# Another spacing of the edge stage's beats, and another order of loads, biases and accumulators in the first node tiles

## The chip, the cores and the metric

The kernel runs on one core of one Trainium2 chip, as one launch. The metric is the device time in microseconds (us). The core has five engines that are programmed apart and meet through semaphores: PE (matmuls), DVE (vector operations), ACT (activations), POOL (here mostly the issue of gathers and scatters) and SP (the issue of plain loads and stores).

## The reference, cut to what matters

The program is two layers on 625 nodes of 1024 numbers and 10000 edges. The change lies in layer 0 alone: a graph attention in 256 hidden numbers and four heads, a linear attention beside it, and a small quantised feed-forward block.

```python
def L0_gnn(x, edge_index, rms_w, W_down, Wl, Wr, att, W_up):
    x = x * rsqrt(mean(x * x) + 1e-6) * rms_w @ W_down
    src, dst = edges and one self loop a node
    xl, xr = (x @ Wl).reshape(n, 4, 64), (x @ Wr).reshape(n, 4, 64)
    msg = xl[src] + xr[dst]
    e = einsum('ehd,hd->eh', where(msg > 0, msg, 0.2 * msg), att)
    alpha = softmax of e over the edges of one dst
    return segment_sum(alpha[..., None] * xl[src], dst).reshape(n, 256) @ W_up

def L0_mix(x, ...):                      # linear attention, 16 heads of 64
    q, k, v = elu(x @ W_q + b_q) + 1, elu(x @ W_k + b_k) + 1, x @ W_v + b_v
    kv, ksum = einsum('bhnd,bhne->bhde', k, v), k.sum(axis=2)
    return (q @ kv / (q @ ksum + 1e-6)) @ W_o + b_o

def L0_ffn(x, w_gate, w_up, w_down):     # activations quantised by row, weights to -1, 0, 1
    return bitlinear(silu(bitlinear(x, w_gate)) * bitlinear(x, w_up), w_down)

xn = layernorm(x)
x = x + L0_gnn(xn, ...) + L0_mix(xn, ...)
x = x + L0_ffn(layernorm(x), ...)
# layer 1 follows: graph convolution twice, linear attention, latent attention, 8 experts of which 2
```

## The kernel before, in words

The nodes are five tiles of 125 (`NT` and `P`). Inside the part that the change touches the order on every engine is the order in which the program is written: `do(prep, pe, after, after2)` emits a group of matmuls and puts off what follows it on DVE and ACT to the next one or two calls of `do`. So a line that stands earlier in the program stands earlier in the queue of its engine, and an engine works its queue in order.

**The edge stage.** The edges are cut into chunks of 128, 79 in all (`EN`), in 40 groups of two (`groups`; the last has one chunk of 16 edges). For each chunk POOL gathers the rows `xl[src]` (L621, tile `ga`) and `xr[dst]` (L621, tile `gb`). For each group DVE adds them, applies the rectifier and `att`, and sums by head (`score_group`, L631 and L601 to L604). ACT takes the exp (L608). For each chunk POOL then scatters the four numbers an edge into `table`, a matrix in DRAM by source and destination (L641). The scatters all write `table`, so each waits until the one before has landed.

How often each pair of nodes occurs is counted meanwhile on PE from one-hot rows that DVE makes (`count`), into `CT`. Attention then needs no edges any more: it multiplies tiles of `table` by tiles of `CT`.

The edge stage runs beside the matmuls of the linear attention: keys and values in two halves (`lin.key`, `lin.value`), then queries and answers (`lin.query`, `lin.answer`), then the output projection (`mixed`, accumulators `px`). Each of these calls `work(us)` with an estimate of its matmul time. When the sum passes the next threshold, `one_beat` emits one beat: it is here that the gathers of group g, the scores of group g - `lags[0]`, the exp of group g - `lags[1]` and the scatters of group g - `lags[2]` are put into the queues, in this order:

```python
                for j in range(G):
                    if g < len(groups):
                        gather(g, j, 0)
                        scatter(g - lags[2] - 1)
                        gather(g, j, 1)
                    scatter(g - lags[2])
```

`scatter` takes the next chunk of the list if its group is old enough, and does nothing otherwise. The first gather of a beat waits for the last matmul that was emitted before it (`behind(got, latest["pe"])`); this is called its gate. The thresholds are 5.2 us apart for six beats and 8.6 after. The lags are 4, 5 and 6 groups, and 1, 1 and 2 from the output projection on; there two scatters fit between the gathers of one `j`, until the backlog is gone. Beats that are left when the matmuls run out follow in `while chunks: one_beat()`, behind the ternary weights of the feed-forward block (`ternary`, three operations on DVE for each of three matrices).

The loads of weights are issued by SP, each behind a matmul group: `lin.ahead[0].load()`, `wo[-1].load()` and `raw` after `lin.answer(m)`. The second half of tile 2's projection, `mixed(2, cs=(1,))`, is put behind the last scatter: it runs once the table is complete.

**The node tiles.** Then come seven periods, `p` from 0 to 6. SP and ACT load `table` by tiles (`load_table(t)`, tile `tb`) and SP the rows of x. In period p: `weigh(p + 1)` multiplies a table tile by the counts (L876, tile `pT`), `sums(p)` and `turn_sums(p)` make the attention's output, `up_again(p)` multiplies it by `W_up` on top of `px` of this tile, and L944 adds it to x. The feed-forward block of tile p - 1 goes through its steps `p1`, `f1` to `f4`, `p5` and `f5`; `f4` is the matmul with `w_down` into `pdn`, and L1042 adds it to x. `add_bias` adds the bias rows `bo` to x (L1069), and for tile 3 the finished projection `kept`. Tile 4's projection is made in period 1 in two halves, and `in_degrees` counts the edges of each node into `pdeg` in period 2.

The accumulators are three pairs of banks (`ps2`: `px`, `pdn`, `pdeg` among others) and two single banks (`ps1`). SBUF holds four tiles of the kind `mid`, which `tb`, `pT`, `kept` and later `kf` and `v` share.

Of the kernel before, what the change touches and what calls it, by code (L numbers as in the profile page):

```python
# [21 lines left out]
P = 125  # L22
# [31 lines left out]
def attempt(ctx: ExitStack, tc: tile.TileContext, w: dict, out: bass.AP, shifted: bool):  # L54
# [8 lines left out]
    def ps1(name):  # L63
        pool, n = psums[-1]
        return pool.tile([128, 512], FP, tag="ps1", name=name, bufs=n)

    def ps2(name):
        return psums[-1][0].tile([128, 2, 512], FP, tag="ps2", name=name, bufs=3)
# [294 lines left out]
    with ExitStack() as st0:  # L363
# [8 lines left out]
        with ExitStack() as edges:  # L372
# [305 lines left out]

            beat = dict(us=0.0, g=0, scored=0, raised=0)
            lags = [4, 5, 6]

            def scores(last):
# [10 lines left out]
            def one_beat():  # L695
                g = beat["g"]
                beat["g"] += 1
                if 5 <= g < NT + 5:
                    self_loops(g - 5)
                if lags[1] > lags[0]:  # L700
                    raise_all(g - lags[1])
                    scores(g - lags[0])
                else:
                    scores(g - lags[0])
                    raise_all(g - lags[1])
# [7 lines that stand above are left out]
            def work(us):  # L713
                beat["us"] += us

                while beat["us"] >= 2.0 + 5.2 * min(beat["g"], 6) + 8.6 * max(beat["g"] - 6, 0) and chunks:
                    one_beat()

            work(0.0)
            states = []  # L720
# [81 lines left out]
            def ternary(i):  # L802
# [4 lines left out]
                nc.vector.tensor_scalar(m, v.rearrange("p (k n) -> p k n", k=m.shape[1]), MAGIC, None,  # L807
                                        op0=ALU.subtract)

            for m in range(KC):  # L810
                if m + 1 < KC:
                    lin.query(m + 1)
                else:
                    mixed(0, range(6), paced=False)
                lin.answer(m, oT)
                if m < 2:
                    lin.ahead[0].load()
                elif m < 6:
                    if m % 2 == 0:
                        wo.append(Half(wpool, w["L0_Wo"], m // 2 - 1, now=False))  # L820
                    wo[-1].load()
                if m < 3:

                    raw.append(mid([128, 2 * D], "raw"))
                    behind(nc.sync.dma_start(out=raw[m].rearrange("p (k n) -> p k n", n=(256, 256, D)[m]),
                                             in_=w[("w_gate", "w_up", "w_down")[m]]
                                             .rearrange("(k p) n -> p k n", p=128)), latest["pe"])
# [3 lines left out]
            dn = mix.tile([128, 2, D], BF, tag="kv", name="dn", bufs=2)  # L831
            gu = wpool.tile([128, KC, 512], BF, tag="w", name="gu", padded_shape=[128, KC, 512])
            made = [gu[:, :, 0:256], gu[:, :, 256:512], dn]
            lags[:] = 1, 1, 2
            kept = mid([P, 2, 512], "kept")
            mixed(3, keep=kept, then=weight_sums)
            mixed(0, range(6, KC))
# [137 lines left out]
        def ffn(t):  # L975

            room = late.tile([128, 1536], FP, tag="room", name="room", bufs=1)
            xq = room[:P, 0:D]
            qT = room[:, D:D + KC * 64].bitcast(BF).rearrange("p (k n) -> p k n", k=KC)
            sg = room[:P, 0:256]  # L980
            hT = room[:, 256:384].bitcast(BF).rearrange("p (k n) -> p k n", k=2)
            xn1 = [mix.tile([128, NP], FP, tag="qf", name="xn1", bufs=2)[:P, 0:512] for h in range(2)]

            def p1():
                stats(t, mv0, rs0)
                nc.vector.tensor_scalar(xq, x[:, t, :], mv0[:, t, 0:1], rs0[:, t:t + 1],
                                        op0=ALU.subtract, op1=ALU.mult)
                quantise(xq, xq, rx[:, t:t + 1])

            def f1():  # L990
                def pe():
                    for h in range(2):
                        p = ps1("ptr").rearrange("p (c n) -> p c n", c=4)
                        for c in range(4):
                            k = 4 * h + c
                            nc.tensor.transpose(p[:, c, :P], xq[:, k * 128:(k + 1) * 128], ident[:P, :P])
                        nc.vector.tensor_scalar(qT[:, 4 * h:4 * h + 4, 0:P], p[:, :, :P], MAGIC, None,
                                                op0=ALU.subtract)

                do(None, pe)  # L1000

            def f2():
                def pe():
                    hold["pgu"] = ps2("pgu")[:, 0, :] if t == NT - 1 else ps1("pgu")
                    group(hold["pgu"][:P], [(qT[:, k, 0:P], gu[:, k, :]) for k in range(KC)])

                def after():
                    pgu = hold["pgu"]
                    rgu = late.tile([P, 2], FP, tag="rgu", name="rgu", bufs=2)

                    nc.vector.tensor_scalar(rgu, wmean[:P, 0:2], rx[:, t:t + 1], None, op0=ALU.mult)
                    nc.vector.tensor_scalar(rgu[:, 0:1], rgu[:, 0:1], 0.5, None, op0=ALU.mult)
                    nc.scalar.activation(sg, pgu[:P, 0:256], AF.Tanh, scale=rgu[:, 0:1])
                    nc.vector.scalar_tensor_tensor(sg, sg, 1.0, pgu[:P, 0:256], op0=ALU.add, op1=ALU.mult)
                    nc.vector.tensor_tensor(rgu[:, 1:2], rgu[:, 0:1], rgu[:, 1:2], op=ALU.mult)
                    nc.vector.scalar_tensor_tensor(sg, pgu[:P, 256:512], rgu[:, 1:2], sg, op0=ALU.mult, op1=ALU.mult)
                    quantise(sg, sg, rh[:, t:t + 1])

                do(None, pe, after)

            def f3():
                def pe():
                    ph = ps1("phT").rearrange("p (c n) -> p c n", c=4)
                    for c in range(2):
                        nc.tensor.transpose(ph[:, c, :P], sg[:, c * 128:(c + 1) * 128], ident[:P, :P])
                    nc.vector.tensor_scalar(hT[:, :, 0:P], ph[:, 0:2, :P], MAGIC, None, op0=ALU.subtract)

                do(None, pe)

            def f4():  # L1030
                def pe():
                    hold["pdn"] = ps2("pdn")
                    for c in range(2):
                        group(hold["pdn"][:P, c, :], [(hT[:, k, 0:P], dn[:, k, c * 512:(c + 1) * 512])
                                                   for k in range(2)])

                def after():
                    rd = late.tile([P, 1], FP, tag="rd", name="rd", bufs=2)
                    nc.vector.tensor_scalar(rd, wmean[:P, 2:3], rh[:, t:t + 1], None, op0=ALU.mult)
                    for c in range(2):  # L1040
                        xc = x[:, t, c * 512:(c + 1) * 512]
                        nc.vector.scalar_tensor_tensor(xc, hold["pdn"][:P, c, :], rd, xc, op0=ALU.mult, op1=ALU.add)  # L1042

                do(None, pe, after)

            def p5():
                stats(t, mv1, rs1)
                for h in range(2):
                    nc.vector.tensor_scalar(xn1[h], x[:, t, h * 512:(h + 1) * 512], mv1[:, t, 0:1], rs1[:, t:t + 1],
                                            op0=ALU.subtract, op1=ALU.mult)  # L1050

            def f5():
                def pe():
                    for h in range(2):
                        p = ps1("ptr").rearrange("p (c n) -> p c n", c=4)
                        for c in range(4):
                            nc.tensor.transpose(p[:, c, :P], xn1[h][:, c * 128:(c + 1) * 128], ident[:P, :P])
                        nc.scalar.activation(xnT1[:, 4 * h:4 * h + 4, nodes(t)], p[:, :, :P], AF.Copy)  # L1058

                do(None, pe)  # L1060

            return p1, f1, f2, f3, f4, p5, f5
# [8 lines left out]
        load_table(0)  # L1071
        for t in range(NT):
            rows_dma(nc.sync, x[:, t, :], xrows[t])
            if t == 1:
                load_table(1)
        weigh(0)
        add_bias(0, 1)
        kv_pieces = iter([(f, t) for t in range(NT) for f in ("key", "value")])
        made_of = {}

# [15 lines left out]
        for p in range(NT + 2):  # L1096
# [3 lines left out]
            if 1 <= p <= NT:  # L1100
                made_of[p - 1] = ffn(p - 1)
                made_of[p - 1][0]()
            if p == 1:
                mixed(4, cs=(0,))
            if p == 2:
                add_bias(2, 4)
                in_degrees()
            if p >= 3:
                spacer()
# [22 lines left out]
                weigh(p + 1)  # L1132
            if p + 2 < NT:
                load_table(p + 2)
            if p == 1:
                add_bias(3)
            if p == 1:
                mixed(4, cs=(1,))
                lin1.weights(0)
# [868 lines left out]
```

## Time and profile before

| | us |
|---|---|
| median of three runs | 2176.61 (2176.5 to 2177.32) |
| profiled execution, whole | 2173.66 |
| profiled execution, span from the first to the last instruction | 2171.8 |
| PE busy | 2094.0 (96% of the span) |
| DVE busy | 711.9 |
| POOL busy | 328.4 |
| ACT busy | 194.8 |
| edge stage, from the first gather to the last scatter | 51.97 to 404.85 |
| seven periods of node tiles | 405.9 to about 599 |

All times inside the execution are counted from its first instruction. The table is read so: PE works nearly all the time, so the end of the program moves by what PE waits less or more; busy time of the other engines counts only where PE waits for them. Durations come from the one profiled execution, and are compared with its own time.

A beat is named by its group number g, from 0. In the program before, beats 26 to 35 stand in the queries, beats 36 to 39 in the output projection and two more, with scatters alone, behind the ternary weights.

### The profile page before, as it was taken

To read this page: it belongs to the slowest core of one execution; us is meant where nothing else is said; L and a number is where in the kernel's file an instruction comes from. 1 tells how busy PE (TensorE), PEld (TensorE's weight loads), DVE (VectorE), ACT (ScalarE), POOL (GpSimd) and SP (SyncE) were. 2 spreads that over 40 slices of the span, in tenths; PEclk is the share of its full clock that TensorE was granted. 3 is DMA by queue.
4 is the path that set the end of the run, shared out by engine and by line. 5 is a ranking of instruction groups with operands and counts; after the bars stand their busy time and mean duration, and the time that the engine had idled before them with its cause. 6 is when DMAs were issued, how large, how long until landed. Compare 5 with 4: busy or idle time off the path is not lost. (4 is left out here: it accounts for less than half of the span.)

```text
span 2171.8 us, 17390 instructions
## 1 busy us (share of the span) xinstructions
PE 2094.0 (96%) x6934; PEld 1198.0 (55%) x6934; DVE 711.9 (33%) x1214; ACT 194.8 (9%) x355; POOL 328.4 (15%) x329
## 2 busy tenths in 40 slices
PE   8999999499999999999999999999999999999998
PEld 6665674255446677744446776467644444444443
DVE  5786486666443720000031334212111111111012
ACT  2000110012111100000000111110000000000000
POOL 1777766200000202010000000100000000000011
PEclk9999999699999999999999999999999999999999
DMA  7632362440302202131203101122299978997832
GB/s 224 206 112 83 118 199 75 120 134 1 120 6 78 84 5 87 49 136 42 75 1 125 59 0 40 35 90 97 82 366 342 328 276 323 330 328 265 293 136 86
DMA packets 147925, 301.63 MB, mean 139 GB/s; under 512 B 12411, under 2 KB 25602, under 8 KB 147830
## 3 DMA queue, kind: packets, MB, share of 16 engines
q1 hardware_dynamic: 127548, 252.54, 33.1%
q0 software_dynamic: 15296, 37.61, 5.5%
q10 hardware_dynamic: 4986, 10.22, 1.5%
q8 instruction: 58, 0.95, 0.2%
q14 instruction: 37, 0.30, 0.0%
HBM read 277.49 MB, written 22.84 MB: 138 GB/s over the span
## 5 line engine op out<-in xcount | busy, mean ns | idle before, releaser
L137 PE MATMUL pu<-w,xgT 128*128 128x512 f32 x768 | 333.9, 593 | 1.9 <-DVE xgT L1302 1.9
L137 PEld LDWEIGHTS pu<-w,xgT 128*128 128x128 f32 x768 | 144.0, 190 | 174.8 <-issue 172.0
L137 PE MATMUL pyb<-w,hb 128*128 128x512 f32 x384 | 174.3, 598 | 2.5 <-ACT yb L105 2.1
L137 PE MATMUL pk<-w,xnT 128*125 128x512 f32 x320 | 143.7, 603 | 2.2 <-ACT xnT L1058 2.2
L137 PE MATMUL pv<-w,xnT 128*125 128x512 f32 x320 | 140.8, 593 | 0.9 <-DVE x L944 0.9
L137 PE MATMUL pq<-xnT,w 128*128 128x313 f32 x512 | 139.3, 431 | 1.0 <-DVE v L293 0.8
L137 PE MATMUL p<-tT,w 128*128 128x313 f32 x512 | 136.3, 428 | 0.4 <-DVE tT L1302 0.4
L137 PEld LDWEIGHTS pq<-xnT,w 128*128 128x128 f32 x512 | 97.8, 192 | 40.5 <-DVE v L293 1.6
L137 PEld LDWEIGHTS pyb<-w,hb 128*128 128x128 f32 x384 | 69.8, 189 | 90.9 <-issue 74.8
L1842 DVE TENSOR_TENSOR su<-pu,su 128x512 f32<-128x512 f32 x24 | 16.6, 691 | 314.6 <-ACT su L1841 314.6
L137 PEld LDWEIGHTS p<-tT,w 128*128 128x128 f32 x512 | 96.8, 190 | 37.9 <-issue 1.2
L137 PEld LDWEIGHTS pk<-w,xnT 128*125 128x125 f32 x320 | 60.3, 191 | 76.0 <-issue 73.3
L765 PE MATMUL px<-w,oT 128*125 128x512 f32 x160 | 72.5, 611 | 30.9 <-DMA table<-es,at 28.4
L137 PEld LDWEIGHTS pv<-w,xnT 128*125 128x125 f32 x320 | 59.5, 188 | 73.5 <-issue 71.2
L641 POOL DMA_INDIRECT table<-es,at x79 | 83.8, 1061 | 56.4 <-issue 26.7
L1825 POOL DMA_INDIRECT xg<-rows_d,slots x12 | 11.3, 945 | 524.8 <-PE pxg L1832 449.0
L621 POOL DMA_INDIRECT ga<-xl_d,si x79 | 81.3, 1030 | 30.2 <-issue 21.7
L621 POOL DMA_INDIRECT gb<-xr_d,di x79 | 80.5, 1019 | 25.3 <-issue 23.5
L1191 DVE TENSOR_TENSOR z<-pz,z 125x512 fp32r<-125x512 f32 x10 | 6.9, 692 | 196.8 <-ACT z L1189 196.8
L137 PE MATMUL px<-w,hT 128*125 128x512 f32 x160 | 70.3, 592 | 0.0
L137 PE MATMUL px<-w,oT 128*125 128x512 f32 x160 | 70.3, 592 | 0.0
L137 PE MATMUL ph<-meanT,w 128*128 128x313 f32 x256 | 70.1, 426 | 0.0
(362 smaller groups left out, 2478.4 us busy)
## 6 DMA issues: line engine op xcount, KB each, us to landing
w<-in_eW_dram SPq DMA_DIRECT2D x144, 1024.0 KB
w<-in_L_Wk_dram SPq DMA_DIRECT2D x8, 1024.0 KB
w<-in_L_Wv_dram SPq DMA_DIRECT2D x8, 1024.0 KB
w<-in_L_Wq_dram SPq DMA_DIRECT2D x8, 1024.0 KB
w<-in_L_Wo_dram SPq DMA_DIRECT2D x8, 1024.0 KB
w<-in_W_self_dram SPq DMA_DIRECT2D x8, 1024.0 KB
w<-in_W_neigh_dram SPq DMA_DIRECT2D x8, 1024.0 KB
w<-in_sW_dram SPq DMA_DIRECT2D x8, 1024.0 KB
```

The source lines that it names most:

```text
L137: made = nc.tensor.matmul(dst, lhsT=lhsT, rhs=rhs, start=(i == 0), stop=(i == len(pairs) - 1))
L621: got = nc.gpsimd.indirect_dma_start(out=ab[g][side][0:p, j, :], out_offset=None, in_=src[:, :], in_offset=bass.IndirectOffsetOnAxis(ap=ix ...
L641: put = nc.gpsimd.indirect_dma_start(out=table[:, :], out_offset=bass.IndirectOffsetOnAxis(ap=at[0:p, lo + j:lo + j + 1], axis=0), in_=es[ ...
L765: made = nc.tensor.matmul(hold["px", t][:P, c, :], lhsT=oT[:, k, nodes(t)], rhs=wo[c](k), start=(k == 0), stop=(k == KC - 1 and keep is no ...
L1191: nc.vector.tensor_tensor(low, src, high.bitcast(FP), op=ALU.subtract)
L1825: nc.gpsimd.indirect_dma_start(out=xg, out_offset=None, in_=rows_d[:, :], in_offset=bass.IndirectOffsetOnAxis(ap=slots[:, b:b + 1], axis=0))
L1842: nc.vector.tensor_tensor(su, pu[:, 0, :], su, op=ALU.mult)
```

## The change

It has five parts.

- The thresholds of the beats: the next one is kept in `beat["next"]`. After six beats they are 8.3 us apart while keys and values are made, 8.6 in the queries, 7.0 in the output projection.
- The last lags are 1, 1 and 1.
- `load_table(1)` is issued after the rows of tile 0 instead of after those of tile 1.
- The biases of tiles 1 to 4 are all added in period 1, behind `p1` of tile 0; before, tile 1's stood ahead of the periods, tile 3's later in period 1 and those of tiles 2 and 4 in period 2.
- In `f4` tile 0 takes two single banks for `pdn` instead of a pair.

In the order of the program this moves beats 10 to 40 forward in part: beats 22 to 24 by one key or value, beat 27 from query 1 to the states before it, beats 28 and 29 by one query each, beats 32 to 34 likewise, beat 36 from tile 3's projection to `answer(6)`, beats 37 to 39 by half a tile's projection or one. Beat 36, which had the short lags before, has the long ones now. The two beats that stood behind the ternary weights become one with two scatters inside tile 1's projection, one with two inside tile 2's, and one with a single scatter at the end.

```diff
-            beat = dict(us=0.0, g=0, scored=0, raised=0)
+            beat = dict(us=0.0, next=2.0, apart=8.3, g=0, scored=0, raised=0)
...
             def work(us):
                 beat["us"] += us
 
-                while beat["us"] >= 2.0 + 5.2 * min(beat["g"], 6) + 8.6 * max(beat["g"] - 6, 0) and chunks:
+                while beat["us"] >= beat["next"] and chunks:
                     one_beat()
+                    beat["next"] += 5.2 if beat["g"] <= 6 else beat["apart"]
...
+            beat["apart"] = 8.6
             for m in range(KC):
                 if m + 1 < KC:
                     lin.query(m + 1)
...
-            lags[:] = 1, 1, 2
+            lags[:] = 1, 1, 1
+            beat["apart"] = 7.0
             kept = mid([P, 2, 512], "kept")
...
             def f4():
                 def pe():
-                    hold["pdn"] = ps2("pdn")
+                    if t:
+                        both = ps2("pdn")
+                        hold["pdn"] = [both[:P, c, :] for c in range(2)]
+                    else:
+                        hold["pdn"] = [ps1("pdn1")[:P] for c in range(2)]
                     for c in range(2):
-                        group(hold["pdn"][:P, c, :], [(hT[:, k, 0:P], dn[:, k, c * 512:(c + 1) * 512])
+                        group(hold["pdn"][c], [(hT[:, k, 0:P], dn[:, k, c * 512:(c + 1) * 512])
                                                    for k in range(2)])
...
         load_table(0)
         for t in range(NT):
             rows_dma(nc.sync, x[:, t, :], xrows[t])
-            if t == 1:
+            if t == 0:
                 load_table(1)
         weigh(0)
-        add_bias(0, 1)
+        add_bias(0)
...
             if p == 1:
+                add_bias(1, 2, 3, 4)
                 mixed(4, cs=(0,))
             if p == 2:
-                add_bias(2, 4)
                 in_degrees()
...
-            if p == 1:
-                add_bias(3)
             if p == 1:
                 mixed(4, cs=(1,))
                 lin1.weights(0)
```

More of the change, by code (lines that the diff above doesn't have):

```diff
@@ L1041, in after @@
                         xc = x[:, t, c * 512:(c + 1) * 512]
-                        nc.vector.scalar_tensor_tensor(xc, hold["pdn"][:P, c, :], rd, xc, op0=ALU.mult, op1=ALU.add)
+                        nc.vector.scalar_tensor_tensor(xc, hold["pdn"][c], rd, xc, op0=ALU.mult, op1=ALU.add)
                 do(None, pe, after)
```

## The prediction

> **What bounds the kernel now.** I read the busy shares first (PE 96%), then the waits of PE, because only time in which PE stands still can be won. Each line names who waited, for what, the sum, the times and the longest, in us.
>
> ```profile
> PE px L765 <- DMA table<-es,at: 28.4, 1, 28.4
> PE px L765 <- DVE x L944: 2.4, 1, 2.4
> PE pdeg L137 <- DVE x L1042: 1.5, 1, 1.5
> PE pdn L137 <- DVE x L944: 1.3, 1, 1.3
> ```
>
> The 28.4 is the edge stage: tile 2's second half cannot start before the last of 79 scatters has landed. The other three lie in the first node tiles. These four are what the change can reach.
>
> Next the timeline of POOL, which issues the edge stage's 158 gathers and 79 scatters (start, length, idle before and who ended it), with the SP queue's timeline at the same place.
>
> ```profile
> 261.93 0.96 POOL L621 DMA_INDIRECT ga<-xl_d,si  x1 [0.48 <-PE pq L137]
> ...
> 264.45 0.98 POOL L641 DMA_INDIRECT table<-es,at  x1 [0.30 <-issue]
> ...
> 270.75 1.40 POOL L641 DMA_INDIRECT table<-es,at  x1 [2.80 <-DVE ga L631]
> 272.47 0.96 POOL L621 DMA_INDIRECT ga<-xl_d,si  x1 [0.32 <-PE pq L137]
> ```
>
> ```profile
> 263.80 0.37 SPq L124 DMA_DIRECT2D w<-in_L_Wq_dram  x1
> 264.26 0.47 SPq L825 DMA_DIRECT2D raw<-in_w_gate_dram  x1
> ```
>
> A gather costs 0.96 and a gap of 0.30, a scatter 0.98 and 0.30; a beat of two times "gather, gather, scatter" is 7.62. Every scatter also waits until the scatter before has landed, since both write `table`. Two 1 MB loads start at 263.8, the scatter of 264.45 lands behind them, and the next goes at 270.75 instead of 268.28. The same is seen after the loads at 274.3, 284.9 and four later ones. Almost no gather waits for its PE gate: after 76 us the first gathers of beats 27, 28 and 29 alone are put down to PE, and POOL would have been free 0.18, 0.02 and 0.01 before them (the end of the scatter before, plus 0.30). So POOL's issues and landings set the pace, not the beats.
>
> The end of the stage, same timeline:
>
> ```profile
> 345.61 0.99 POOL L641 DMA_INDIRECT table<-es,at  x1 [0.30 <-issue]
> 346.90 0.96 POOL L621 DMA_INDIRECT ga<-xl_d,si  x1 [0.30 <-issue]
> 348.51 0.98 POOL L641 DMA_INDIRECT table<-es,at  x1 [0.65 <-issue]
> ...
> 387.77 2.17 POOL L641 DMA_INDIRECT table<-es,at  x1 [0.30 <-issue]
> 391.85 1.81 POOL L641 DMA_INDIRECT table<-es,at  x1 [1.91 <-issue]
> ...
> 398.78 0.96 POOL L641 DMA_INDIRECT table<-es,at  x1 [1.88 <-issue]
> 401.13 0.96 POOL L641 DMA_INDIRECT table<-es,at  x1 [1.40 <-DMA table<-es,at]
> 404.00 0.85 POOL L641 DMA_INDIRECT table<-es,at  x1 [1.91 <-issue]
> ```
>
> From beat 36 (346.90) scatters and gathers alternate; there the landing sets the interval between scatters and the gather between is free. After the last gather (385.19) six scatters go alone, 2.61 apart at the end, 3.74 while DVE's ternaries run (384.83 to 396.07).
>
> Last, DVE in the first node tile:
>
> ```profile
> 417.67 0.69 DVE L1069 TENSOR_TENSOR x<-x,bk_t 125x512 f32<-125x512 f32 x1 [0.99 <-DMA x<-in_x_dram]
> ...
> 423.20 4.89 DVE L876 TENSOR_TENSOR pT<-tb,CT 125x500 f32<-125x500 f32 x5 [2.48 <-DMA tb<-table]
> 427.99 1.23 DVE L944 TENSOR_TENSOR x<-px,x 125x1024 f32<-125x1024 f32 x1
> ```
>
> The second table tile lands at 423.20; `weigh(1)` holds DVE until 428.0; L944, whose input PE had ready at 426.83, comes behind it and gives back the accumulator for which tile 4's matmuls (429.28) wait.
>
> **What the Trainium skill says.** "DMA: Bandwidth & Descriptors", section "Anatomy of one DMA", puts the fixed cost of a POOL-issued DMA at about 2.0 us, mostly the receipt: the trace has 2.1 us to landing as the median for the scatters, and up to 6.3 beside loads. Its section "Issuing engines are not separate DMA queues" says that all queues interleave on the same 16 engines; the 2.5 us lost at 264.45 agrees. "SBUF — State Buffer", section "SBUF: two separate sides", says that a DVE operation in a two-port mode keeps GpSimd from writing descriptors; the trace agrees, with issues of 2.27, 2.17, 1.81 and 1.83 beside the ternaries. "PSUM — Partial Sum Buffer", section "Specifications", has eight banks per partition: three pairs and two singles fill them, so a fourth pair must wait for one to come free, as `pdn` does here (1.3).
>
> **The change, part by part.** *Beats.* The number of gathers, scatters and DVE operations stays. In program order beats 27 to 29 move up one query each, beat 36 moves from tile 3's matmuls to `answer(6)`, and the last ones follow. What this takes away is the gate: 0.2 us by the three numbers above. The loads hang on PE and stay, and a scatter behind a load leaves when the load is done, however early it came; that fixes POOL's time again at each load. Only a scatter that slips ahead of a load wins, a whole 3.81; it needs POOL about 2.3 us earlier there, and from 225.22 to 260.46 all slowdown together is 0.95 (35.24 against nine times 3.81). I take 0 for this, with 0 to -7.6 as bounds (two such slips). So beat 36 starts at 346.7 to 346.9 as before.
>
> *Last lags.* Beat 36 now comes before the lags are shortened and keeps "gather, gather, scatter". Its scatters go at +2.54 and +6.36 instead of +1.61 and +4.50, and the next at 356.15 instead of 354.31: 1.84 later. Seventeen scatters are then left in either kernel, two more of them alone (eight after the last gather, not six): alternating, an interval is 2.82 (348.51 to 383.81, twelve, less one stall of 1.51), alone 2.61, so 0.4 is won. Together with the gates: 1.84 - 0.4 - 0.2 = **+1.2**. Group 39's scores no longer stand behind the ternaries; that saves nothing, since its exp was ready at 397.7 and its scatter went at 404.00. The ternaries now wait for gather 39, which I put near 383, and start near 385 as before; their cost on POOL I keep, with -2 to +7 as bounds (nothing overlapped more; all 11.3 us of them overlapped, of which 4.5 is paid already). New wait: beat 38's scores stand before `kept` on DVE and wait for gather 37 (some 366), so `kept` ends near 370 instead of 363.6; tile 2's first half waits for that accumulator from 370.5. If it is late, the 28 us wait covers it.
>
> *Loads.* The two table DMAs of `load_table(1)` pass x tile 1's two on SP. Tile 1 took 2.28 us to land after tile 0 (417.67 - 415.39), so the table lands 2.3 earlier, at 420.9, and x tiles 1 to 4 up to 5.5 later (estimate: tile 4 at 430, used at 437). `weigh(1)` ends at 425.8, L944 starts when PE is done (426.87), tile 4's matmuls at 428.16: **-1.12**.
>
> *Biases.* Ten DVE additions, 0.61 apart, eight of them now together behind tile 0's quantising: 433.5 to 438.4, where DVE idled 6.1 us until `dens` (440.76, then 439.6). Cost nothing; if tile 4 landed after 438, it would delay `dens` by as much. Gone are two ahead of hT's copy (L1026) and four at 466.9 to 469.4, which held nobody. `kept` comes free earlier, so table tile 3 takes its place and waits for the additions (438.4) instead of PE (440.7); POOL's two bias loads (63.6 us of waiting) and the memset behind move from 469 to 439. Nothing waits for these before 478.
>
> *Accumulators.* For tile 0 `pdn` gets the single banks of `pgoT` and `phT`, the latter free with hT's copy, for which it waits anyway (452.5 now). It follows `px` at 3.44, as at 482.43 to 485.87: 453.67 instead of 456.26, of which 1.12 is counted: **-1.47**. `pdeg` then takes the pair of `px` 1, free when L944 ends (455.1) instead of L1042 (458.74): 455.15 instead of 458.79, **-1.05** more. Next in line are the transposes of `xn1`; DVE has those ready at 459.6, PE needs them at 462.2. From there PE has waits of 0.6 at most for two tiles, so the 3.64 reaches the end.
>
> Sum: 1.2 - 3.64 = -2.4. The profiled execution took 2173.66 (span 2171.8 and 1.9 around it), hence 2171.3; the three runs' median, 2176.61, lies 2.95 above it, hence 2174.2. About 0.2%, 4.35 us, is what a measurement of this kernel tells from no change.
>
> **Rivals.** *One: a scatter slips ahead of a load.* For it: one slip keeps its 3.81, and the old gates at beats 27 to 29 would have taken it back. Against it: 0.95 us to win, 2.3 needed. One slip gives -6.2, two -10.0; middle 2169.0. *Two: the lone scatters meet the ternaries and end slower than before.* Place: POOL, 378 to 406. Each lone scatter beside ternaries costs 3.74 instead of 2.61. It decides from 2.4 us, that is two more scatters caught; at four more it is +4.5 - 2.4 = +2.1, 2178.7, at the bound +7 - 2.4 = +4.6. Against it: DVE starts the ternaries at nearly the same time. *Three: the node tiles' waits move on instead of going* (DVE's stats before tile 1's transposes become the bound) and the change does nothing there: +1.2, 2177.8. Against it: 2.6 us of slack.
>
> **Chances.** Forecast 0.52 (2171.5 to 2176, a tenth of it below -4.35), one 0.29, two 0.12 (a third of it above +4.35), three 0.07. Faster 0.34, same 0.61, slower 0.05. The range, 2166.5 to 2178.5, takes in two slips and most of rival two.
>
> **What would show it.** Right: gathers still put down to "issue" at 260 to 345; beat 36 within 1 us of 346.9; eight lone scatters; the last scatter near 405; PE's waits on L944 near 1.3 and none for `pdn`; `pdeg` 3.6 earlier after the stage's end. Wrong: the last scatter before 402, or PE waits elsewhere between 455 and 500.

## The result, and the profile after

| | kernel before | changed kernel |
|---|---|---|
| median of 20 runs each, us | 2176.56 (2172.33 to 2180.14) | 2171.19 (2167.68 to 2176.42) |
| ratio | | 0.9976, 95% interval 0.9969 to 0.9984 |
| profiled execution, whole, us | 2173.66 | 2175.02 |

The change makes the kernel faster by about 5 us (5.4 by the medians). The profiled execution of the changed kernel is one of its longer ones, so the two profiles do not show that gain as a difference of their ends. They are compared by stage, each from its own mark: the first gather, and **M**, PE's start on tile 2's second half, right after the last scatter (405.94 before, 407.87 after). A time written M+17.46 is one 17.46 us after M in its own execution.

First the waits of PE from 400 to 520 us, after (who waited, for what; sum, times, longest):

```profile
PE px L766 <- DMA table<-es,at: 28.0, 1, 28.0
PE px L766 <- DVE x L947: 2.6, 1, 2.6
...
PE pg L137 <- ACT xnT L1065: 1.3, 2, 1.1
...
PE pdeg L137 <- DVE x L947: 0.5, 1, 0.5
```

Of the four waits shown before, that of `pdn` (1.3) is gone and that of `pdeg` is cut from 1.5 to 0.5. The one for L944 (now L947) stays: 2.6 against 2.4. A new one has come up, for ACT's copy of the transposes, 1.1 against 0.4 at its longest.

The timeline of POOL after, from beat 36 on (start, length, idle before and who ended it):

```profile
348.70 0.97 POOL L621 DMA_INDIRECT ga<-xl_d,si  x1 [0.30 <-issue]
...
356.07 1.36 POOL L641 DMA_INDIRECT table<-es,at  x1 [0.30 <-issue]
357.73 0.96 POOL L621 DMA_INDIRECT ga<-xl_d,si  x1 [0.30 <-issue]
359.34 1.16 POOL L641 DMA_INDIRECT table<-es,at  x1 [0.65 <-issue]
...
382.67 0.86 POOL L621 DMA_INDIRECT gb<-xr_d,di  x1 [0.31 <-issue]
383.83 1.00 POOL L641 DMA_INDIRECT table<-es,at  x1 [0.30 <-DMA table<-es,at]
386.76 2.28 POOL L641 DMA_INDIRECT table<-es,at  x1 [1.93 <-ACT es L608]
...
405.94 0.85 POOL L641 DMA_INDIRECT table<-es,at  x1 [1.91 <-issue]
```

The last gather is at 382.67 instead of 385.19, and eight scatters follow alone instead of six. The last scatter comes 1.94 later, of which 0.48 is a later first gather (52.45 against 51.97).

DVE after, in the first node tile:

```profile
425.33 4.87 DVE L879 TENSOR_TENSOR pT<-tb,CT 125x500 f32<-125x500 f32 x5 [2.64 <-DMA tb<-table]
430.11 1.22 DVE L947 TENSOR_TENSOR x<-px,x 125x1024 f32<-125x1024 f32 x1
```

Table tile 1 lands at M+17.46 (before: 423.20, M+17.26), though its DMAs now stand ahead of x tile 1's. L947 is as late as it was. SP's queue shows how little the new place is worth: the two DMAs of table tile 1 are issued at M+6.86 before (412.80) and at M+6.09 after (413.96), 0.77 earlier.

```profile
412.80 0.87 SPq L180 DMA_DIRECT2D tb<-table  x2
```

```profile
413.96 0.85 SPq L180 DMA_DIRECT2D tb<-table  x2
```

PE in period 2, first before, then after:

```profile
456.26 1.02 PE L137 MATMUL pdn<-dn,room 128*125 128x512 bf16 x4 [1.31 <-DVE x L944]
458.79 7.17 PE L137 MATMUL pdeg<-CT,ones 125*128 125x313 f32 x20 [1.50 <-DVE x L1042]
465.80 1.02 PE L1057 MATMUL ptr<-ident,xn 125*128 125x125 f32 x8
467.23 4.58 PE L137 MATMUL pg<-xl,pT 125*125 125x65 f32 x40 [0.41 <-ACT xnT L1058]
...
475.35 7.03 PE L137 MATMUL pk<-w,xnT 128*125 128x512 f32 x16
```

```profile
456.89 1.03 PE L137 MATMUL pdn<-dn,room 128*125 128x512 bf16 x4
458.37 5.54 PE L137 MATMUL pdeg<-CT,ones 125*128 125x313 f32 x20 [0.45 <-DVE x L947]
463.75 1.02 PE L1064 MATMUL ptr<-ident,xn 125*128 125x125 f32 x8
465.85 7.10 PE L137 MATMUL pg<-xl,pT 125*125 125x65 f32 x40 [1.08 <-ACT xnT L1065]
...
474.83 3.37 PE L137 MATMUL pgu<-gu,room 128*125 128x512 bf16 x8
...
478.25 7.03 PE L137 MATMUL pk<-w,xnT 128*125 128x512 f32 x16
```

From M, `pdn` starts 1.30 earlier than before and `pdeg` 2.35 earlier. `pdeg` also runs in 5.54 us instead of 7.17. Then `pg` takes 7.10 us and `pgu` 3.37; the windows view says why (window, its length; busy time and instructions of PE, PEld, DVE, ACT and POOL; granted PE clock, DMA share, GB/s):

```profile
470.00:480.00 10.00, 9.82 (x38) 7.00 (x38) 3.60 (x11) 2.03 (x3) 0.00 (x0) 0.61 0.50 125
467.57:477.81 10.24, 10.06 (x42) 8.29 (x41) 3.04 (x8) 1.28 (x1) 0.00 (x0) 0.50 0.38 100
```

PE was granted 0.61 of its clock over those 10 us, and half of it from 467.57 to 477.81. `pk` (478.25) starts 70.38 after M, against 69.41 before: in this execution the clock has taken back all that the accumulators had won.

### The profile page after: what moved, and what is told of

The parts are those of the page before. It is cut to its first block, busy times and chain, and to the rows that moved or that the text cites. A ratio compares the mean times of both kernels' runs of the same rounds, so it can differ in the third digit from the quotient of the medians.

```text
span 2173.3 us, 17398 instructions
## 1 busy us (share of the span) xinstructions
PE 2096.6 (96%) x6934; PEld 1202.3 (55%) x6934; DVE 712.4 (33%) x1214; ACT 194.4 (9%) x355; POOL 327.6 (15%) x329
## 5 line engine op out<-in xcount | busy, mean ns | idle before, releaser
L766 PE MATMUL px<-w,oT 128*125 128x512 f32 x160 | 72.8, 612 | 32.2 <-DMA table<-es,at 28.0
L766 PEld LDWEIGHTS px<-w,oT 128*125 128x125 f32 x160 | 30.4, 193 | 72.0 <-issue 36.9
```

Source lines behind the costliest of these rows:

```text
L766: made = nc.tensor.matmul(hold["px", t][:P, c, :], lhsT=oT[:, k, nodes(t)], rhs=wo[c](k), start=(k == 0), stop=(k == KC - 1 and keep is no ...
```

## The experiments

Theories: **A**, POOL's issues and landings bound the edge stage, and the node tiles give the gain. **B**, the gain comes from the beats, through the gates. **C**, falls of PE's clock make the changed kernel's times scatter. The experiments ran on three chips. On the chip of e5 to e8 the kernel before took 2175.91 us (39 runs); on those of e1 to e4 and e9 to e12 it took 2201.65 (51 runs) and 2202.82 (56 runs), the edge stage being longer in the profiles taken there (first gather to M 367.9 to 386.5, against 352.2 to 355.4). Each ratio is to the kernel before on the same chip.

### The two parts apart: e1, e10 (beats) and e2, e9 (node tiles)

Beats and last lags alone:

```diff
-                while beat["us"] >= 2.0 + 5.2 * min(beat["g"], 6) + 8.6 * max(beat["g"] - 6, 0) and chunks:
+                while beat["us"] >= beat["next"] and chunks:
                     one_beat()
+                    beat["next"] += 5.2 if beat["g"] <= 6 else beat["apart"]
...
-            lags[:] = 1, 1, 2
+            lags[:] = 1, 1, 1
+            beat["apart"] = 7.0
```

Node part alone: the other hunks of the change (loads, `add_bias`, `pdn`) on the old beats.

> The kernel before with the new thresholds and last lags alone. Theory A (POOL's issues and landings bound the edge stage, the gates do not): the last scatter 1 to 2 us later than before, eight scatters alone after the last gather, and the time 0 to 2 us above before. Rival B (the earlier beats are what brought the gain): the last scatter 3 us or more earlier, and the time 3 to 5 us below before.

> Kernel before with the beats and last lags alone, as e1. Theory A, as forecast: eight lone scatters, the edge stage from the first gather to PE's start on tile 2's second half 1 to 1.5 us longer than with the old beats (354.0 in the profile of before), time 0 to 1.5 us higher, ratio 1.000 to 1.0007. Rival B: ratio 0.9975 to 0.999. Theory G (the beats make no difference that can be measured; loads met by chance spread the stage by 3 us whatever the beats): ratio 0.9993 to 1.0005, stage within 352 to 356 in both.

> The kernel before with the loads, biases and accumulators of the node tiles alone. Theory A: the edge stage as before (last scatter within 0.5 us relative to the first gather), PE's wait for pdn gone, pdeg 2.3 us earlier counted from the end of the edge stage, no gain from the table's load; time 4 to 8 us below before, since the edge stage's loss is not there either. The span between pdeg and the keys of period 2 shows whether PE's clock falls there. Rival B: within 1.5 us of before.

> Kernel before with the node part of the change alone (loads, biases, accumulators), as e2, which ran where every kernel took 25 us more and told nothing by its time. Theory A: the node part carries the whole gain; from the start of PE on tile 2's second half to the end of the span 1760.7 us (1765.9 in the kernel before), so 4 to 5.5 us less and a ratio of 0.9975 to 0.998; pdeg 5.4 us long at full clock. Rival B (the beats bring the gain): ratio 0.999 to 1.000.

Measured: the beats alone 1.0003 (0.9991 to 1.0015) and 1.0008 (0.9993 to 1.0022); the node part alone 0.9999 (0.9985 to 1.0013) and 0.9982 (0.9971 to 0.9994). On these two chips B falls as the source of the gain: in neither comparison do the beats win anything. Of the node part only the second comparison shows a gain; e2 had been expected 4 to 8 us below before. Both parts were timed only on the two chips with the longer edge stage; by the means of all runs the beats make +0.7 us (of +1.8 and -0.4) and the node part -2.2 (of -4.2 and -0.3), together some -1.5, give or take 2.7 (95%); the whole made -3.7 in e3, which this does not tell apart.

The traces tell more, from M, since nothing of the edge stage is in it. With the old node part `pk` starts at M+69.41 (before), 69.98 (e1) and 71.54 (e10); with the new one at 66.43 (e2) and 69.28 (e9). All that follows M is the same code in most of the runs below too, so their profiles can be put together. From M to the end of the span it takes 1765.8, 1766.4 and 1766.3 us with the old node part (before, e1, e10). With the new one it takes 1760.6, 1760.7, 1760.7 and 1760.7 (e3, e4, e5, and e6 with its later loads), 1762.9 (e2), 1764.6 (e8), 1765.4 (after) and 1766.5 (e9): 3.4 less in the mean. In the first four of these PE's clock does not fall between M+30 and M+300; in the other four it does. So the node part is worth some 5 us where no fall follows, and about nothing where one takes it back, as in e9, where 1760.7 had been expected.

On these two chips POOL did wait for PE's gates. The gathers' waits beyond the usual 0.30 add up to 41.2 and 36.2 us with the old beats (e2, e9) and 20.6 and 28.5 with the new (e1, e10), against 7.8 in the profile of before; PE ended 34 and 27 us of the former and 13 and 16 of the latter. So the gates do cost something where PE comes late. The edge stage differs as well: from the first gather to M it takes 383.1 to 386.5 with the old beats (e2, e9, e11) and 372.6 to 378.0 with the new (e1, e3, e10, e12), where e10 had been expected at 352 to 356. But no gain from it shows in the times, and the profiles may mislead here: the three with old beats lie 3.5 to 6.2 us above the median of their kernel, the four with new beats 5.6 to 7.0 below. On the chip of e5 to e8 the beats were not timed alone.

### The changed kernel once more: e3, e5

> The changed kernel once more, for its two groups of times (near 2168.5 and near 2175). Theory C (a fall of PE's granted clock between pdeg and the keys of period 2 makes the difference): a profiled execution near 2175 shows a clock near 0.6 at 470 to 480 us and pgu at 3.4 us, one near 2168.5 shows full clock there and pgu at 2.0. Rival D (a scatter that slips ahead of a load makes it): the last scatter differs by 3.8 us between the two groups, and the clock at 470 to 480 is the same in both.

> The changed kernel once more, beside e6 to e8 on one chip; the measure for those three. In the first comparison the changed kernel was 0.9976 of the kernel before, in the second (on a chip where every kernel took some 25 us more) 0.9988. Theory A (POOL's issues and landings bound the edge stage, the node tiles give the gain) and rival B (the gates give it) both expect 0.997 to 0.999. Theory C (the 20 times of the changed kernel fall in two groups because PE's granted clock falls at period 2 in some executions): in this run's profile either pgu takes 1.97 us and pk starts at M+65.5 to 66 (M = start of PE on tile 2's second half), or it takes over 3 us and pk starts near M+70; in the first case the time is 3 to 5 us lower. Without C the two have nothing to do with each other.

Measured: 0.9988 (0.9973 to 1.0003) and 0.9982 (0.9975 to 0.9989). The same stretch of PE in e5 as shown above for after:

```profile
454.41 1.03 PE L137 MATMUL pdn<-dn,room 128*125 128x512 bf16 x4
455.89 5.54 PE L137 MATMUL pdeg<-CT,ones 125*128 125x313 f32 x20 [0.45 <-DVE x L947]
463.36 4.58 PE L137 MATMUL pg<-xl,pT 125*125 125x65 f32 x40 [1.08 <-ACT xnT L1065]
469.45 1.98 PE L137 MATMUL pgu<-gu,room 128*125 128x512 bf16 x8
```

The program is the same and so are the waits, but `pg` takes 4.58 and `pgu` 1.98 at full clock. `pk` starts at M+66.23, 4.15 earlier than in the profile of after; e3 too shows no fall there (M+65.89). So one fall of the clock is worth 4 us, and a given program may or may not meet it: the falls of C are real. The clock recorded for each run says the same: of the 20 times of the changed kernel in the first result the eight shortest (to 2169.30) all have 0.989 as the mean clock, the nine longest (from 2172.49) 0.985 to 0.988. Two separate groups of times, as C put it, are not there: but for one at 2180.34 the 22 times of e5 spread from 2167.69 to 2176.63 with no step of more than 1.1. The time to M, which has nothing to do with this, differs too: from the first gather to M 352.21 in e5, 353.43 in e6, 355.32 in e7 and 355.42 in after, with the same edge code.

### Shorter lags: e4, e8

```diff
                 lin.answer(m, oT)
+                if m == 3:
+                    lags[:] = 4, 4, 4
```

> The changed kernel with all three lags at 4 from answer 3 on, so that scatters catch up earlier and three instead of eight stand alone after the last gather; everything else as in the change. Theory A: each scatter that no longer stands alone saves up to 1.3 us, less 0.3 for each pair that alternates, so the last scatter comes 3 to 6 us earlier than in the changed kernel and the time falls by as much. Rival B (the gates and beats set the end): no change beyond 1 us. If DVE has to wait for gathers under the shorter lag, PE shows waits in the queries, and the gain is lost.

> Changed kernel, with the lags cut to 4,4,4 from the answer to query 3 on (as e4_short_lags, 0.9967 there): fewer scatters are left alone at the end. Theory A: three to five lone scatters instead of eight, last scatter 4 to 9 us earlier than in e5's profile, time 3 to 8 us lower than e5, ratio to before 0.994 to 0.996. Rival B (PE's pace and gates bound the stage): shorter lags make POOL wait for DVE's scores in the middle, the last scatter is at most 1 us earlier, the time equals e5's.

Measured: 0.9967 (0.9952 to 0.9982) on e4's chip, 0.9987 (0.9978 to 0.9995) on e5's, where it is no better than the changed kernel. POOL in e8:

```profile
326.12 0.98 POOL L641 DMA_INDIRECT table<-es,at  x1 [2.41 <-DMA table<-es,at]
...
331.74 1.40 POOL L641 DMA_INDIRECT table<-es,at  x1 [3.31 <-DMA table<-es,at]
...
342.89 0.98 POOL L641 DMA_INDIRECT table<-es,at  x1 [2.25 <-DMA table<-es,at]
...
393.47 0.86 POOL L621 DMA_INDIRECT gb<-xr_d,di  x1 [0.31 <-issue]
...
405.45 1.79 POOL L641 DMA_INDIRECT table<-es,at  x1 [1.90 <-issue]
```

Four scatters are left after the last gather, not eight, and from beat 36 to the last scatter it takes 45.15 us, not some 57. But beat 36 itself comes 306.94 after the first gather (293.37 in e5): the scatters pulled forward wait for landings beside the loads instead. M comes 354.97 after the first gather, within the 352.21 to 355.42 of the others. A lag moves a scatter's landing; it does not remove it. That is theory A, but A's forecast of 3 to 8 us was wrong. PE waited as well, 9.5 us for `kept` (`px L766 <- DVE kept L775`), inside the time that it would have stood waiting for the last scatter. On e4's chip, where POOL waits for gates anyway, scatters pulled forward may fill those waits: from the first gather to M e4 takes 367.9, e3 377.8. That was not tested further, and e4's profile is the shortest of its 14 executions.

### Table tile 1's landing: e6, e12

Theory **E**: table tile 1 gains nothing because the x tiles behind it share the DMA engines with it. **F**: its landing takes as long whatever runs beside it. e6 holds the x tiles behind it back until PE has done tile 2's second half; e12 until DVE has done its first product with table tile 1, and takes e7's edit too:

```diff
 # e6
-            rows_dma(nc.sync, x[:, t, :], xrows[t])
+            for put in rows_dma(nc.sync, x[:, t, :], xrows[t]):
+                if t:
+                    behind(put, latest["pe"])
 # e12: only x tile 0 ahead of load_table(1); tiles 1 to 4 after weigh(1)
+            if p == 0:
+                for t in range(1, NT):
+                    for put in rows_dma(nc.sync, x[:, t, :], xrows[t]):
+                        behind(put, hold["weighed"])
```

> Changed kernel, with the loads of x tiles 1 to 4 held on SP until PE has done tile 2's second half, so that table tile 1 has only table tile 0 and x tile 0 beside it. Theory E (table tile 1 gained nothing because the x tiles behind it on SP share the DMA engines with it): its 1.22 MB lands at M+14 to 15.5 instead of M+17.5, PE's wait on L947 falls from 2.6 to 1.3 us or less, PE's px for tile 4 starts 1.1 to 1.3 earlier, the time is 1.1 to 1.3 lower than e5. Rival F (the strided read of the table itself takes some 11 us from issue to landing, whatever runs beside it): landing stays at M+17 to 17.5, no change of time. If the x tiles land after M+30 the additions on DVE are late and dens with them: 1 to 3 us slower.

> Changed kernel with the late copy of the in-degrees (as e7), and with the loads of x tiles 1 to 4 moved behind the first product of table tile 1, so that beside table tile 1's 1.22 MB there are only table tile 0 and x tile 0 (in e6 the x tiles still started 2 us after it). Theory E (sharing of the DMA engines with the x tiles held it up): it lands at M+14.5 to 15.5 (M+15.9 to 17.8 in the runs of the same order so far), PE's wait on L947 is 1.3 us, PE waits nowhere for x. Rival F (it takes 11 us from its issue whatever is beside it): M+17. If the x tiles come after M+30, dens and tile 4 are late and the time rises by up to 2 us. Against e7 (0.9965): the same or up to 1 us lower.

Measured: e6 0.9978 (0.9968 to 0.9987), table tile 1 at M+17.23; in e6 the x tiles still started 2.8 us after it, and they were on their way while it was. PE's wait was 1.32 all the same, and e6 is no faster than e5 by more than the intervals. The short wait is no gain: PE came later itself. Here is the same place before, then in e5, where the wait is 1.32 too:

```profile
421.74 5.09 PE L939 MATMUL px<-wu,goT 128*125 128x512 f32 x8 [0.53 <-ACT goT L927]
429.28 7.13 PE L765 MATMUL px<-w,oT 128*125 128x512 f32 x16 [2.45 <-DVE x L944]
```

```profile
420.94 6.64 PE L942 MATMUL px<-wu,goT 128*125 128x512 f32 x8 [0.53 <-ACT goT L930]
428.91 7.13 PE L766 MATMUL px<-w,oT 128*125 128x512 f32 x16 [1.32 <-DVE x L947]
```

The eight matmuls ahead of the wait took 6.64 us in e5 (6.43 and 6.42 in e3 and e6) instead of 5.09, since the clock was at half there for 6.83 us and not for 3.41. What is left of the wait, 1.32, is L947's own 1.22 on what these matmuls made. Tile 4's matmuls start at M+23.66 in e5, 23.31 in e3 and 23.29 in e6, against 23.34 before.

e12 gave 0.9967 (0.9952 to 0.9982). The table tile in e12, and PE behind it (M is 428.91):

```profile
444.82 4.89 DVE L879 TENSOR_TENSOR pT<-tb,CT 125x500 f32<-125x500 f32 x5 [0.90 <-DMA tb<-table]
450.17 1.22 DVE L949 TENSOR_TENSOR x<-px,x 125x1024 f32<-125x1024 f32 x1 [0.47 <-PE px L944]
```

```profile
451.45 7.13 PE L766 MATMUL px<-w,oT 128*125 128x512 f32 x16 [1.32 <-DVE x L949]
```

Alone with table tile 0 and x tile 0 it lands at M+15.9, and PE waits 1.32, as E said; with the eight matmuls ahead at 5.20 us, tile 4's start at M+22.54, and this is the one run where the early tile clearly gains. Where nothing holds the x tiles back it landed at M+15.9 (e5), 16.3 (e3, e9), 16.4 (e4), 17.1 (e7), 17.5 (after) and 17.8 (e2, e8); with the old order of loads at 17.3 (before), 17.8 (e1, e11) and 18.1 (e10). So neither theory has it whole: beside the x tiles it lands up to 2 us later in most executions, not in all, and without them it still takes 9.5 us from its issue (435.30), later than E put it.

### The in-degrees' copy: e7

```diff
-            do(None, pe, lambda: nc.scalar.activation(halves(degree), hold["pdeg"][:, :, :HN], AF.Copy))
+            do(None, pe, lambda: None, lambda: nc.scalar.activation(halves(degree), hold["pdeg"][:, :, :HN], AF.Copy))
```

> Changed kernel, with ACT's copy of the in-degrees (int16) put off by one slot, so that the copies of tile 1's transposes come first on ACT. Theory C: PE's wait of 1.08 us for ACT ahead of pg(2) shrinks to about 0.5; with less of a hole there the clock falls less often, so the times have fewer in the upper group and the median is 0.5 to 2 us below e5; the profile shows pgu at 1.97. Rival (the clock falls for a reason outside this place, for instance the transposes of 1 to 2 us[...]): the wait shrinks by about 0.5 us, the two groups stay as they are, and the median is at most 0.5 us below e5.

Measured: 0.9965 (0.9952 to 0.9978), 2169.01 as the median of 5 runs, beside e5's 2171.55. ACT's queue in after shows what was in the way: the copy of 0.67 us stands ahead of the transposes' copies.

```profile
464.64 0.67 ACT L1101 ACTIVATE degree<-pdeg 128x626 int16<-128x626 f32 x1
465.21 1.06 ACT L1065 ACTIVATE xnT<-ptr 128x500 f32<-128x500 f32 x2
```

In e7 they are the other way round, and PE waits 0.50 instead of 1.08:

```profile
465.35 4.58 PE L137 MATMUL pg<-xl,pT 125*125 125x65 f32 x40 [0.50 <-ACT xnT L1065]
```

`pg` starts at M+57.03, 1.08 earlier than in e5. The wait shrank by 0.58 as foreseen. e7 and e12, which has the edit too, have the lowest ratios on their chips. Whether their clock falls less often cannot be told from the profiles: neither shows the fall, but of the nine profiles with the wait of 1.08 or 1.09 only three (after, e9, e11) show it there. The recorded clocks speak for it: their mean is 0.9898 over e7's 5 runs and 0.9882 over e5's 22. Of a time of 2170 us the difference would be some 3.5 us (estimate: 0.0016 times 2170), and the means of the times differ by 3.0. With 5 runs this is a sign and not a proof; e7 differs from e5 in nothing but this edit.

### The accumulators alone: e11

Only `f4`'s hunk on the kernel before: tile 0's `pdn` in two single banks.

> Kernel before with tile 0's pdn in the two single banks and nothing else of the change. Theory H (the accumulators alone carry the node part's gain, in part through PE's clock: with the waits of 1.3 and 1.5 us ahead of pdn and pdeg gone, pdeg runs in 5.4 instead of 7.0 us): pdn starts 1.3, pdeg 2.4 us earlier after the start of tile 2's second half, pk 3 to 4 us earlier, ratio 0.998 to 0.9985. Rival I (the short pdeg needs the loads' and biases' order as well): pdeg stays at 7 us, pk 1.5 to 2.5 us earlier, ratio 0.9988 to 0.9995.

Measured: 0.9993 (0.998 to 1.0006), with this in the profile (M is 438.65):

```profile
489.45 5.54 PE L137 MATMUL pdeg<-CT,ones 125*128 125x313 f32 x20 [0.33 <-DVE x L944]
...
496.93 6.67 PE L137 MATMUL pg<-xl,pT 125*125 125x65 f32 x40 [1.09 <-ACT xnT L1062]
...
505.48 3.62 PE L137 MATMUL pgu<-gu,room 128*125 128x512 bf16 x8
```

`pdn` comes 0.93 and `pdeg` 2.05 earlier after M than in the profile of before, and `pdeg` runs at full clock, as H said (5.54 us). H's `pk` 3 to 4 us earlier and its ratio of 0.998 to 0.9985 were not met: the clock falls where it fell in after, and `pk` starts at M+70.66 (M to the end: 1766.8). So this hunk alone removes the wait of `pdn` and most of `pdeg`'s; whether it alone gives the time is open.

## Why the prediction was right, and where its steps were wrong

The forecast was 2174.2 with 2166.5 to 2178.5, and -2.4 us for the change. The runs gave about -5, -4 and -4 us (first result; e5 and e3 by their means). Faster by over 0.2% had a chance of 0.34; no measurable change, at 0.61, was held likelier. That the sum came near is in part luck: a loss of 1.2 in the edge stage and a part of the 3.64 in the node tiles both failed to come, and a gain that the forecast has no term for did.

- **Gates and slips, 0.2 and 0.** Kept, on the chip of the profile: the gathers' waits beyond 0.30 add up to 6.4 us after and 7.8 before. Beat 36 starts 296.25 after the first gather (294.93 before), but 293.37, 294.76 and 296.83 in e5, e6 and e7: the same code spreads by 3 us there. In e5 a scatter did slip ahead of the loads: of the 79 scatters the one that waits 3 us behind the two loads of 264.7 (265.3 in e5) is the 44th in after and the 45th in e5; POOL is 5.5 us ahead at beat 28 and 2.9 at beat 36. So rival one's slip does happen and is worth up to 3 us here; but it came in one execution of a program and not in the next, and nothing shows that the change brings it.
- **Last lags, +1.84 - 0.4.** Both terms were mis-sized, and they cancel. From beat 36 to its third scatter it takes 10.64 us (359.34) where before it took 7.41 (354.31): +3.2. The sixteen intervals that are left take 46.60 instead of 49.69: -3.1. Half of that is the stall of 1.51 at 363.17 that the forecast had taken out of the old interval and that does not come back. From beat 36 to the last scatter it took 57.10, 57.34, 57.65 and 57.33 with the old lags (before, e2, e9, e11), and 57.24, 56.90, 56.74 and 56.55 with the new (after, e5 to e7). The cost is about 0 (-0.5 by the two means), not 1.44. The eight lone scatters are there, three of them long beside the ternaries (2.28, 2.33 and 1.83); rival two, slower by these, did not come.
- **Table tile 1, -1.12.** This is the step that failed on the node side. I let its landing move by as much as x tile 1 had taken to land, 2.28. Its issue moved by 0.77 only, and the queue is no order of landing: after its issue the x tiles share the DMA engines, as the Trainium skill says in "DMA: Bandwidth & Descriptors", section "Issuing engines are not separate DMA queues", which I cited and did not apply here. PE's wait behind it was 2.6 (after) and 2.9 us (e2), 1.6 in e7 and 1.3 in e3, e5 and e6, against 2.4 before. But in the last three PE was as late itself, and tile 4's matmuls start 0.32 later than before to 0.05 earlier from M (0.18 later in after, 0.18 earlier in e7). So the -1.12 came to about 0 in the changed kernel; only e12, which holds the x tiles back, starts them 0.80 earlier.
- **Biases, 0.** Kept: eight additions from 436.67 to about 441.6, and `dens` (442.87, M+35.0; before M+34.8) not held up. PE waited 1.6 us for `kept`, as was thought possible; that lay inside the time that it would have waited for the last scatter, so it cost nothing.
- **`pdn` -1.47, `pdeg` -1.05.** Right. `pdn` starts 1.30 (after) and 1.16 (e5) earlier from M, though tile 4's matmuls ahead of it start 0.18 and 0.32 later: -1.48 in both. `pdeg` gains 1.05 more in both.
- **"From there PE has waits of 0.6 at most for two tiles".** Wrong by one place: I looked at DVE for what would be late next. It was ACT, with the in-degrees' copy ahead of `xnT`'s: the wait grew from 0.41 to 1.08 (+0.67), of which e7 takes 0.58 away.

PE stands still for 8.3 us in the first 80 us from M before, 6.3 after and 5.9 in e5 (80 less the busy time of eight windows). So the waits give 2.0 to 2.4 us of the 3.64, and with the edge at about 0 the waits alone make the sum again near -2. **The other 2 to 3 us** do not come from any term of mine: I put the clock at nothing. What differs besides waiting is the clock. One fall goes with the waits: `pdeg` took 7.17 and 7.23 us behind stops of 1.31 and 1.50 in before and e1, and 5.54 in all eleven profiles with the new accumulators (but also in e10, with the old). Others move from run to run, to M+60 or M+150.

From M to the end, with every stretch at half clock taken at its own length, the sum closes: in all fourteen profiles the time is 1716.8 to 1717.6 us, plus what PE stands still, plus what the clock takes. In the mean the three with the old node part stand still for 39.1 us and lose 9.8 to the clock, the eight with the new 36.3 and 9.3. Of the 3.4 us between them the waits make 2.8 and the clock 0.5; without e10, where the clock came back early after M and PE waited longer, it is 1.7 and 1.4 of 3.3. Within the eight the clock's part goes from 7.9 to 12.4, so a share of this size may be chance. From before to e5 the two are 3.2 and 1.4 of 5.1. The recorded clocks of the runs on e5's chip fit: 0.98774 in the mean of 39 runs before, 0.98818 in e5's 22, which is about 1 us of the 4 (estimate: 0.00044 times 2170; 95% interval -0.4 to 2.4). So the waits carry half of the gain or more, and whether the new order meets fewer falls, for about 1 us, stays open.

The Trainium skill describes such a pattern for another kernel, in "TensorE: Matmul & The Clock Gate", section "A second HAM failure mode: psum-queue depth-cycling": frequent short stops between groups of matmuls make the clock swing. The trace agrees in part: in the 36 us ahead of the fall at 467.57 PE had stood still for no longer than 1.08 us at a time. But e5 has the same stops and no fall.

Against both kernels: the changed kernel with e7's edit (0.9965), and with e12's as well (0.9967), have the lowest ratios of those that keep the whole change, beside e4 (0.9967, but 0.9987 when repeated as e8); e7 rests on 5 runs, e12 on 11.

## What to carry to other kernels

A wait that is removed is worth its length only up to the next engine in line: look in every queue that feeds the next matmul, ACT's small copies too, before counting on slack. A transfer put ahead in one queue is not alone on the DMA engines; what it gains is set by what runs beside it, and a shorter wait behind it is a gain only if the matmuls start earlier too. And before a few us are put down to an edit, take two or three profiles of one kernel: here the same program differed by 3 us in one stage and by 4 us at one fall of the clock.

## What the runs showed of the hardware

- In the traces of these runs the granted clock over the first 200 us from M is either full or half. A fall to half lasts 3.41, 6.83 or 10.24 us. The one of 10.24 us in after came when no single stop in the 36 us ahead of it had been longer than 1.08 us, and `pk` came 4.15 us later than in e5; whether it came varied between executions of one program.
- After the wait of 27 to 28 us the clock was at half for the first 5.08 us from M in after and 4.59 in e5 (3.05 in e9), then full for 10.24 us (20.48 in e9), and then at half once more for 3.41 us in after and e9 and 6.83 in e5. The windows of after, in which the granted clock is the third number from the end:

```profile
407.87:412.95 5.08, 5.08 (x6) 2.14 (x7) 0.99 (x2) 0.00 (x0) 0.00 (x0) 0.50 0.81 207
412.95:423.19 10.24, 9.31 (x53) 6.42 (x51) 5.98 (x10) 0.00 (x0) 0.00 (x0) 1.00 0.98 225
423.19:426.60 3.41, 2.89 (x4) 1.33 (x5) 1.27 (x2) 1.66 (x2) 0.00 (x0) 0.50 1.04 238
```

- Where the clock came back early, PE met the table tile's landing sooner and the second fall later. In e9, e8 and e10 (at half for the first 3.05, 3.40 and 2.91 us) the wait on L944 or L947 was 3.75, 5.04 and 5.14, and tile 4's 16 matmuls took 8.83, 8.83 and 10.16 us instead of 7.13.
